# A two-layer network on one core: a row's first stages traced in small pieces between scan items, with chained small matmuls

## The chip, the cores and the metric

The kernel runs on one core of one Trainium2 chip. The metric is the device time of one execution in microseconds (us). Three runs of the kernel before gave 4264.85 to 4278.79 us, with a median of 4274.81 us. The profile is of one more execution, which took 4252.41 us.

The engines are named as the profile does: PE (TensorE, matmuls; PEld its weight loads), DVE (VectorE), ACT (ScalarE), POOL (GpSimd), SP (SyncE, which issues most DMAs). Each takes its own instructions in order and waits for the others on semaphores.

## The reference, cut to what matters

The input `x` has 8 rows of 512 time steps by 256 channels. Two layers add to it four times:

```python
x = x + mamba(ema_gate(x, ...), ...)         # thread X: per row, rows independent
x = x + moe_top2(per_row_linear(x, id7))     # thread Y, first half
x = x + attention(lora_ffn(x, id7), ...)     # thread Y, second half
x = x + moe_top4(per_row_adapter(x, id6))    # top4
```

`ema_gate` has one moving average of the input, a gate, eight modulated moving averages over time that are blended, and a layer norm. `mamba` has a short convolution over time and then a state scan, for 512 channels with 16 states each:

```python
h   = exp(delta[:, None, :] * A) * h + delta * B_t * x_t    # for each of 512 time steps
y_t = einsum('bn,bnd->bd', C_t, h) + D * x_t
```

`lora_ffn` is a two-layer perceptron of 1024 hidden units whose weights get a low-rank correction that depends on the row. `attention` has 8 heads with 64 channels for queries and keys and 256 for values; softmax is over 512 keys. Everything is in float32, apart from a few exact splits into three bfloat16 parts.

## The kernel before, in words

Tiles are 128 channels (or 128 states) on partitions by 512 time steps. A framework traces the kernel as Python, and a scheduler then puts the traced instructions of each engine into an order, by what is ready by its own reckoning of durations and by how early it was traced. The order is fixed when the program is built.

**Thread X** (`thread_x`, L367) does the first addition, row by row. The first stages of a row are `head_a` (L442: gate, eight modulations L475 to L484, layer norm to L513) and `head_b` (L519: convolution L531, gate product, step sizes `dd` by a softplus L559 to L574). The results go to DRAM (`xzs` L535 and L541, `packs` L575). `scan` (L612) then takes the row in 64 items (j, g, k), each 128 lanes of 32 channels by 4 states:

- `begin` (L619) makes the decay `dA` on ACT (L623, Exp) and the input `h` on POOL (L625) from a `packed` tile that a DMA brought (L595); there are 4 buffers for `dA`, 8 for `h`, 5 for `packed`;
- `run` (L645) makes the recurrence on DVE (`tensor_tensor_scan`, L651) and multiplies by C (L652); C comes once per 4 items from a matmul into `c4` (one buffer);
- `add` (L654) folds four items: each item's 4 states are summed by a matmul with a 128x32 matrix into its 32 partitions of `yp` (L660). After the fourth group of states L664 (DVE) and L665 (POOL) make the output `y8`.

`begin` runs two items ahead of `run`. At the end of a row come the product with `W_out`, the sum into `xr` (L685) and the store to `xa` (L686). While row b is scanned, `scan` lets the generator `head(b+1)` advance two steps for each two items; before item 58 it runs that head to its end (`yield from after[0]`). `split3` (L328) makes the three bfloat16 parts.

**Thread Y** (`thread_y`, L711) takes a group of rows, `GROUPS = [[0], [1, 2], [3, 4, 5], [6, 7]]`. It routes tokens to 8 experts (scatters L160 on POOL), runs expert tiles (weights `fw`, L782 to L808), gathers (L323), and then per row does the perceptron (low-rank products into `g`, corrections L838 and L845, products with `wi` and `wo`) and the attention: for each pair of heads, `scores` (L883) makes two products with 64 contracted rows each, the maximum (L893), Exp on ACT with the sum (L896), the reciprocal (L897) and the scaling (L898) on DVE. `turn` transposes (L906, L907), and L923 multiplies by the values; L927 adds to the row.

**Interleaving.** Y of group q is traced while X makes the rows of group q+1. Each generator yields a cost, and the loop at the end of the kernel draws from X as often as keeps the two shares level: `XROW` 269 for a row of X, `YROW` 242 for a row of Y. `filling` (L144) adds DRAM zero fills between X's steps. After X, the last group's Y is traced with the routing of `top4`; then come the top-4 expert tiles and the last gather.

The four folds and the two score products use different column or row groups of the array. Nothing but the trace order keeps them together:

```python
for k in range(4):
    nc.tensor.matmul(
        yps[j][32 * k : 32 * k + 32, :], fold, hs.pop(i + k), start=(g == 0), stop=(g == 3))
```

Of the kernel before, what the change touches and what calls it, by code (L numbers as in the profile page):

```python
# [10 lines left out]
F32 = mybir.dt.float32  # L11
# [6 lines left out]
P = 128  # L18
NB = 8
# [16 lines left out]
XROW, YROW, YGROUP, YTILE, P4ROW = 269.0, 242.0, 20.0, 9.0, 10.0  # L36
# [15 lines left out]
def adaln_attn_ffn_kernel(ctx: ExitStack, tc: tile.TileContext, d: dict, out: bass.AP):  # L52
# [102 lines left out]

    members = {}
# [12 lines left out]
    SYNC = mybir.DependencyInfo(mybir.DependencyClass.Sync, mybir.DependencyReason.DATA)  # L169

# [157 lines left out]
    def split3(pool, src, outs, p0, p1):  # L328

        r = pool.tile([P, T], F32, tag="tr", name="s3_r", bufs=2)[p0:p1, :]  # L330
        m = pool.tile([P, T], BF16, tag="s3_m", name="s3_m")[p0:p1, :]
        nc.scalar.copy(outs[0], src)
        nc.vector.tensor_tensor(r, src, outs[0], ALU.subtract)
        nc.scalar.copy(m, r)
        nc.gpsimd.tensor_tensor(r, r, m, ALU.subtract)
        nc.scalar.copy(outs[1], m)
        nc.scalar.copy(outs[2], r)
# [29 lines left out]
    def thread_x(wp, wk, ps):  # L367
# [74 lines left out]
        def head_a(b):  # L442

            x = rows[b]
            pt = gx()
            mm(pt[:64, :], [(Wn1[:, k, :], x[:, k, :]) for k in range(KC)])
            h1 = wk.tile([64, T], F32, tag="sg", name="h1", bufs=2)
            nc.scalar.activation(h1, pt[:64, :], AF.Gelu, bias=col("bn1", p=64))
            yield 3
            pt = gx()  # L450
            mm(pt[:8, :], [(Wn2, h1)])
            m8 = wk.tile([8, T], F32, tag="tr", name="m8", bufs=2)
            nc.scalar.activation(m8, pt[:8, :], AF.Sigmoid, bias=col("bn2c", p=8))
            split3(wk, m8, [m3[0:8, :], m3[32:40, :], m3[64:72, :]], 0, 8)
            yield 4
            ct = wk.tile([P, KC, T], F32, tag="ct", name="ct")
            for k in range(KC):
                nc.vector.tensor_tensor_scan(
                    ct[:, k, :], alpha[:, 0:1].to_broadcast([P, T]), x[:, k, :], 0.0, ALU.mult, ALU.add)
                yield 1.3  # L460
            gated = wk.tile([P, KC, T], F32, tag="gated", name="gated")
            for e in range(KC):
                pt = gx()
                mm(pt, [(Wg[:, k, ts(e, P)], x[:, k, :]) for k in range(KC)]
                   + [(Wg[:, KC + k, ts(e, P)], ct[:, k, :]) for k in range(KC)])
                sg = wk.tile([P, T], F32, tag="sg", name="sg", bufs=2)
                nc.scalar.activation(sg, pt, AF.Sigmoid, bias=col("bg", e))
                nc.gpsimd.tensor_tensor(gated[:, e, :], x[:, e, :], sg, ALU.mult)
            yield 4
            temporal = wk.tile([P, KC, T], F32, tag="ct", name="temporal")  # L470
            for i in range(8):
                pt = gx()
                mm(pt, [(three[0:72, i : i + 1].to_broadcast([72, P]), m3)])
                gm = wk.tile([P, KC, T], F32, tag="gm", name="gm")
                nc.vector.scalar_tensor_tensor(gm, rep(pt, KC), 0.5, gated, ALU.add, ALU.mult)  # L475
                yield 1.5
                for k in range(KC):
# [8 lines left out]
                    yield 2.2  # L486
            soma = wk.tile([P, KC, T], F32, tag="gm", name="soma")
            for e in range(KC):
                pt = gx()
                mm(pt, [(Wsoma[:, k, ts(e, P)], x[:, k, :]) for k in range(KC)])  # L490
                nc.scalar.activation(soma[:, e, :], pt, AF.Gelu, bias=col("bsoma", e))
            yield 3
            for e in range(KC):
                pt = gx()
                mm(pt, [(Wtemp[:, k, ts(e, P)], temporal[:, k, :]) for k in range(KC)])
                sg = wk.tile([P, T], F32, tag="sg", name="sg", bufs=2)
                nc.scalar.activation(sg, pt, AF.Sigmoid, bias=col("btemp", e))
                nc.gpsimd.tensor_tensor(soma[:, e, :], soma[:, e, :], sg, ALU.mult)
            yield 3
            cen = wk.tile([P, KC, T], F32, tag="cen", name="cen")  # L500
            sq = wk.tile([P, KC, T], F32, tag="gated", name="sq")
            for e in range(KC):
                pt = gx()
                mm(pt, [(Wout[:, k, ts(e, P)], soma[:, k, :]) for k in range(KC)])
                nc.scalar.copy(cen[:, e, :], pt)
                nc.scalar.activation(sq[:, e, :], pt, AF.Square)
                yield 2
            pt = gx()
            mm(pt, [(onesdiv, sq[:, k, :]) for k in range(KC)])
            rstd = wk.tile([P, T], F32, tag="sg", name="rstd", bufs=2)  # L510
            nc.scalar.activation(rstd, pt, AF.Ln, bias=epst)
            nc.scalar.activation(rstd, rstd, AF.Exp, scale=-0.5)
            nc.vector.tensor_tensor(cen, cen, rep(rstd, KC), ALU.mult)  # L513
            yield 3
            rows[b] = cen
            if b + 1 < NB:
                get_row(b + 1)

        def head_b(b):  # L519

            cn = rows[b]
            xc = wk.tile([P, 4, T], F32, tag="xc", name="xc")
            for j in range(4):
                pt = gx()
                mm(pt, [(W_in[:, k, ts(j, P)], cn[:, k, :]) for k in range(KC)])
                xp = xps[j % 2]
                nc.scalar.activation(xp[:, 3:], pt, AF.Identity, bias=wb[:, j : j + 1])
                cv = xc[:, j, :]
                nc.scalar.activation(cv, pt, AF.Identity, scale=col("convw", 4 * j + 3), bias=cb[:, j : j + 1])
                for i in range(3):  # L530
                    nc.vector.scalar_tensor_tensor(  # L531
                        cv, xp[:, i : i + T], col("convw", 4 * j + i), cv, ALU.mult, ALU.add)
                yield 3
            nc.scalar.activation(xc, xc, AF.Silu)
            nc.sync.dma_start(xzs[b % 2][:, :, 0, :], xc)  # L535
            for j in range(4):
                pt = gx()
                mm(pt, [(W_in[:, k, ts(4 + j, P)], cn[:, k, :]) for k in range(KC)])
# [3 lines left out]
            yield 5  # L542
            pt = gx()
            mm(pt[:96, :], [(W_x[:, j, :], xc[:, j, :]) for j in range(4)])
            dt = wk.tile([64, T], F32, tag="dt", name="dt")
            nc.scalar.copy(dt, pt[:64, :])
            bc3 = wk.tile([96, T], BF16, tag="bc3", name="bc3", bufs=2)
            split3(wk, pt[64:96, :], [bc3[64:96, :], bc3[32:64, :], bc3[0:32, :]], 64, 96)
            yield 3

            for j2 in range(2):
                dds, es = [], []
                for j in (2 * j2, 2 * j2 + 1):
                    pt = gx()
                    mm(pt, [(W_dt[:, ts(j, P)], dt)])

                    dd = wk.tile([P, 2, T], F32, tag=("gated", "ct")[j % 2], name="dd")
                    e = wk.tile([P, T], F32, tag="sg", name="sp_e", bufs=2)
                    nc.scalar.activation(e, pt, AF.Abs, bias=col("bdt", j))  # L559
                    nc.vector.tensor_scalar(dd[:, 0, :], pt, col("bdt", j), 0.0, ALU.add, ALU.max)  # L560
                    nc.scalar.activation(e, e, AF.Exp, scale=-1.0)
                    u = dd[:, 1, :]
                    nc.vector.tensor_scalar(u, e, 1.0, None, ALU.add)
                    nc.vector.scalar_tensor_tensor(e, u, 1.0, e, ALU.subtract, ALU.subtract)
                    dds.append(dd)
                    es.append(e)
                yield 3
                for dd in dds:
                    nc.scalar.activation(dd[:, 1, :], dd[:, 1, :], AF.Ln)
                for j, dd, e in zip((2 * j2, 2 * j2 + 1), dds, es):  # L570
                    u = dd[:, 1, :]
                    nc.gpsimd.tensor_tensor(u, u, e, ALU.subtract)
                    nc.gpsimd.tensor_tensor(dd[:, 0, :], dd[:, 0, :], u, ALU.add)
                    nc.gpsimd.tensor_tensor(dd[:, 1, :], dd[:, 0, :], xc[:, j, :], ALU.mult)  # L574
                    nc.sync.dma_start(packs[b % 2][j], dd)  # L575
                yield 3
            rows[b] = bc3

# [33 lines left out]
        def scan(b):  # L612

            bc3 = rows[b]
            items = [(j, g, k) for j in range(4) for g in range(4) for k in range(4)]
            yps, Cs, hs, dAs, xz = {}, {}, {}, {}, {}
            y8 = wk.tile([P, 4, T], F32, tag="y8", name="y8")

            def begin(i):  # L619
                j, g, k = items[i]  # L620
                t = got[b, j, k]
                dA = wk.tile([P, T], F32, tag="dA", name="dA", bufs=4)
                nc.scalar.activation(dA, t[:, 0, :], AF.Exp, scale=A[:, 4 * j + k, g : g + 1])  # L623
# [6 lines left out]
                if j == 0 and g < 3 and k == 1:  # L630
                    get_B4(b, g + 1)
# [570 lines left out]
```

## Time and profile before

| | |
|---|---|
| median of 3 runs | 4274.81 us |
| profiled execution | 4252.41 us, span 4250.6 us |
| mean granted PE clock | 0.889 |
| 512 scans (L651), DVE | 791.0 us, 1571 ns each |
| 512 products with C (L652), DVE | 330.5 us, 672 ns each |
| 512 decays (L623), ACT | 359.8 us, 720 ns each |
| 256 score products (two records each), PE | 210.7 us busy |
| 128 low-rank products (two records each), PE | 63.4 us busy |
| 256 softmax scalings (L898), DVE | 161.8 us, 634 ns each |
| last sum into `xr` of row 0, 1, ... 7 | 406, 750, 1066, 1404, 1749, 2084, 2616, 2938 us |

The span runs from the first to the last instruction. A float32 matmul has two records, one for each pass; busy time is the union of the records, so matmuls that run side by side count once. "Idle before" is idle time of the engine just ahead of an instruction, with what ended it.

### The profile page before, as it was taken

The page shows a single profiled execution, that of the slowest core. Times are in us where ns is not written, and L with a number is a line of the kernel's source. Part 1 is how long each engine was busy: PE and PEld are TensorE (multiplying, and loading weights), DVE is VectorE, ACT ScalarE, POOL GpSimd, SP SyncE. Part 2 cuts the span into 40 slices and gives each one's busy share as a digit, 9 for nine tenths or more (in the row PEclk, how much of TensorE's full clock was granted, in tenths as well). Part 3 has the DMA queues.
Part 4 walks back from the last instruction along what each step waited for, and adds up shares of the span by engine and source line. Part 5 has one row for each costly group of instructions (what it writes and reads, how often), then busy time and mean ns, then how long its engine had stood idle before and what let it go on. Part 6 is the DMA issues. An engine that isn't in the chain of part 4 may idle for free. (4 is left out here: it accounts for less than half of the span.)

```text
span 4250.6 us, 36891 instructions
## 1 busy us (share of the span) xinstructions
PE 3440.5 (81%) x10964; PEld 1694.3 (40%) x10964; DVE 2670.9 (63%) x4290; ACT 1672.2 (39%) x2741; POOL 1565.8 (37%) x1222
## 2 busy tenths in 40 slices
PE   4556686887687888888758899889988999978994
PEld 2111352332254233333327443333456444436773
DVE  4698957886966686796892547575432454443336
ACT  2535463455366346445433443242223233322222
POOL 0456535434635333433542323231043111134552
PEclk7677798988798898999879999899989999989996
DMA  3235455324456423333346312213043312117776
GB/s 105 101 108 180 187 162 170 106 98 156 177 176 209 135 102 118 134 122 109 139 165 234 122 63 77 68 36 104 15 163 136 93 41 70 36 50 245 248 237 224
DMA packets 159372, 554.78 MB, mean 131 GB/s; under 512 B 27730, under 2 KB 34289, under 8 KB 146756
## 3 DMA queue, kind: packets, MB, share of 16 engines
q1 hardware_dynamic: 135076, 501.35, 35.2%
q0 software_dynamic: 24096, 51.08, 3.3%
q8 instruction: 87, 1.43, 0.1%
q14 instruction: 113, 0.93, 0.1%
HBM read 453.00 MB, written 234.82 MB: 162 GB/s over the span
## 5 line engine op out<-in xcount | busy, mean ns | idle before, releaser
L625 POOL TENSOR_TENSOR h<-packed,B 128x512 f32<-128x512 f32 x512 | 792.5, 1570 | 1054.2 <-PE yp L660 746.7
L651 DVE TENSOR_TENSOR_SCAN h<-dA,h 128x512 f32<-128x512 f32 x512 | 791.0, 1571 | 126.3 <-ACT dA L623 67.2
L623 ACT ACTIVATE dA<-packed,Aexp 128x512 f32<-128x512 f32 x512 | 359.8, 720 | 656.4 <-DVE h L651 446.5
L160 POOL DMA_INDIRECT tok<-ys,to_i x310 | 311.9, 1006 | 497.9 <-DVE ys L808 237.7
L660 PE MATMUL yp<-h,fold 128*32 128x512 f32 x1024 | 349.7, 704 | 156.9 <-DVE h L652 140.6
L923 PE MATMUL acc<-aT,V 128*128 128x512 f32 x1024 | 453.4, 597 | 5.3 <-ACT aT L907 3.2
L160 POOL DMA_INDIRECT tab<-row,si x192 | 197.4, 1028 | 465.5 <-issue 210.5
L652 DVE TENSOR_TENSOR h<-h,c 128x512 f32<-128x512 f32 x512 | 330.5, 672 | 29.0 <-PE c L78 28.2
L923 PEld LDWEIGHTS acc<-aT,V 128*128 128x128 f32 x1024 | 193.2, 191 | 245.9 <-issue 235.1
L78 PE MATMUL acc<-wv,c 128*128 128x512 f32 x512 | 270.2, 642 | 0.4
L78 PE MATMUL g<-qk 64*128 64x512 f32 x512 | 210.7, 681 | 54.9 <-ACT ex L896 28.6
L896 ACT ACTIVATE ex<-g,nm 128x512 f32<-128x512 f32 x256 | 173.8, 684 | 157.5 <-DVE nm L893 157.3
L78 PE MATMUL g<-xT,fw 128*128 128x256 f32 x960 | 233.6, 396 | 2.5 <-ACT h L801 1.9
L893 DVE TENSOR_REDUCE nm<-g 128x1 f32<-128x512 f32 x256 | 165.0, 681 | 100.8 <-PE g L78 100.8
L78 PE MATMUL acc<-fw,h 128*128 128x256 f32 x960 | 221.6, 383 | 3.5 <-DVE ys L808 1.8
L78 PEld LDWEIGHTS g<-xT,fw 128*128 128x128 f32 x960 | 188.0, 201 | 39.4 <-issue 6.8
L78 PEld LDWEIGHTS acc<-fw,h 128*128 128x128 f32 x960 | 182.7, 192 | 41.6 <-issue 12.4
L906 PE MATMUL acc<-ident,ex 128*128 128x128 f32 x1024 | 160.3, 286 | 47.9 <-DVE ex L898 16.2
L906 PEld LDWEIGHTS acc<-ident,ex 128*128 128x128 f32 x1024 | 122.6, 146 | 188.4 <-issue 69.3
L660 PEld LDWEIGHTS yp<-h,fold 128*32 128x32 f32 x1024 | 44.7, 115 | 364.1 <-DVE h L652 208.3
L479 DVE TENSOR_TENSOR_SCAN tr<-alpha,gm 128x512 f32<-128x512 f32 x128 | 181.4, 1435 | 5.0 <-POOL y L665 3.5
L78 PE MATMUL g<-xT,mw 128*128 128x256 f32 x760 | 183.1, 385 | 0.0
(280 smaller groups left out, 5458.3 us busy)
## 6 DMA issues: line engine op xcount, KB each, us to landing
fw<-in_fW SPq DMA_DIRECT2D x60, 1154.0 KB
tab<-zeros SPq DMA_DIRECT2D x32, 2112.0 KB
packed<-pack SPq DMA_DIRECT2D x128, 512.0 KB
mw<-in_mW SPq DMA_DIRECT2D x95, 384.0 KB
tab<-zeros SPq DMA_DIRECT2D x16, 2080.0 KB
xt<-tab SPq DMA_DIRECT2D x95, 264.0 KB
xz<-xzs SPq DMA_DIRECT2D x32, 512.0 KB
pack<-dd SPq DMA_DIRECT2D x32, 512.0 KB
```

The source lines that it names most:

```text
L78: nc.tensor.matmul(o, lhsT, rhs, start=(i == 0), stop=(i == len(pairs) - 1))
L160: i = nc.gpsimd.indirect_dma_start(out=table_, out_offset=bass.IndirectOffsetOnAxis(ap=idx, axis=0), in_=src, in_offset=None, bounds_check ...
L479: nc.vector.tensor_tensor_scan(tr, alpha[:, 1 + i : 2 + i].to_broadcast([P, T]), gm[:, k, :], 0.0, ALU.mult, ALU.add)
L623: nc.scalar.activation(dA, t[:, 0, :], AF.Exp, scale=A[:, 4 * j + k, g : g + 1])
L625: nc.gpsimd.tensor_tensor(h, t[:, 1, :], B4s[b, g], ALU.mult)
L651: nc.vector.tensor_tensor_scan(h, dAs.pop(i), h, 0.0, ALU.mult, ALU.add)
L652: nc.vector.tensor_tensor(h, h, Cs[0], ALU.mult)
L660: nc.tensor.matmul(yps[j][32 * k : 32 * k + 32, :], fold, hs.pop(i + k), start=(g == 0), stop=(g == 3))
L893: nc.vector.tensor_reduce(nm, sp, AX.X, ALU.max, negate=True)
L896: nc.scalar.activation(ex, sp, AF.Exp, bias=nm, accum_out=den)
L906: nc.tensor.transpose(tp[:, m, :], ex[:, ts(m, P)], ident)
L923: nc.tensor.matmul(ys[k], V[:, m, C * u + P * k : C * u + P * (k + 1)], aTs[u][:, m, :], start=(u == 0 and m == 0), stop=(u == 1 and m == 3))
```

## The change

1. `head_a` and `head_b` become one generator `head` of about 66 pieces, ended by a bare `yield` each. A matmul, the ACT step on its result and the next DVE or POOL step mostly lie in successive pieces. `split3` is a generator too. `soma` moves into the modulation loop, `get_row` of the next row too.
2. The scan is one loop over the 512 items of all rows. After each item one piece of the heads is traced, after every twelfth two; the folds, the output sum and the end of a row are put into a table `due` and are traced one or more items later, within the next row's items where they fall there. Before item 58 of a row the heads run on until the next row's first `pack` store is traced (`ready`), not to the end of the head.
3. `in_order` gives each instruction of thread X a dependency without a semaphore on the one traced before it on the same engine: the scheduler may not reorder X's instructions.
4. `chain` does the same for the four folds, for the two score products of a turn, and for the low-rank products, which are now traced alternately for `wi` (rows 0 to 31) and `wo` (rows 32 to 63). The first score product also waits for both Exp of the turn before.
5. The softmax scaling goes from DVE to ACT.
6. Buffers: `lora`, `wi`, `wo` share the buffers of `V`, `aT0`/`aT1`, `wv`/`qk`; in X, `m8` moves to `dt`'s, `soma` to `xc`'s, `xr` to `cen`'s. `XROW` is 256; each item yields 4.

```diff
+    def in_order(X):
+        last = {}
+        while True:
+            n = len(nc.cur_bb.bb.instructions)
+            c = next(X, None)
+            for i in nc.cur_bb.bb.instructions[n:]:
+                if i.engine in last:
+                    tc.add_manual_dep(i, last[i.engine].name, NOSYNC)
+                last[i.engine] = i
+            if c is None:
+                return
+            yield c
...
+    def chain(matmuls):
+        for a, b in zip(matmuls, matmuls[1:]):
+            follow(b, a.ins)
...
             for i in range(8):
                 gm = wk.tile([P, KC, T], F32, tag="gm", name="gm")
-                nc.vector.scalar_tensor_tensor(gm, rep(pt, KC), 0.5, gated, ALU.add, ALU.mult)
-                yield 1.5
+                nc.vector.scalar_tensor_tensor(gm, rep(p0, KC), 0.5, gated, ALU.add, ALU.mult)
+                if i in (3, 4):
+                    p0 = gx()
+                    mm(p0, [(Wsoma[:, c, ts(i - 3, P)], x[:, c, :]) for c in range(KC)])
+                yield
...
+            delta(0)
+            yield
+            next(split)
+            soft1(0)
+            delta(1)
+            yield
+            next(split)
+            soft2(0)
+            soft1(1)
+            yield
...
+            if k == 3:
+                due.setdefault(n + 1, []).append(lambda: add(n - 3))
...
+            chain([nc.tensor.matmul(
+                yps[0][32 * k : 32 * k + 32, :], fold, hs.pop(n + k), start=(g == 0), stop=(g == 3)) for k in range(4)])
+            if g == 3:
+                if j == 0:
+                    y8s[b] = wk.tile([P, 4, T], F32, tag="y8", name="y8")
+                due.setdefault(n + 5, []).append(lambda: gate(b, j, n + 6))
...
+        for n in range(N):
+            b, i = divmod(n, 64)
+            if i == 58 and b + 1 < NB:
+                while b + 1 not in ready:
+                    next(H)
+                    yield 0
+            if n + 2 < N:
+                begin(n + 2)
+            run(n)
+            for f in due.pop(n, ()):
+                f()
+            next(H, None)
+            if i % 12 == 4:
+                next(H, None)
+            yield 4
...
+                    pi, po = g(), g()
+                    ms = []
                     for k in range(KC):
-                        mm(pt[:, ts(k, 256)], [(lora[0:32, ts(k, P)], lora[0:32, C + 256 * w : C + 256 * (w + 1)])])
+                        fi, fo = C + 256 * w, C + 256 * w + P * k
+                        ms.append(nc.tensor.matmul(
+                            pi[:, ts(k, 256)], lora[0:32, ts(k, P)], lora[0:32, fi : fi + 256], start=True, stop=True))
+                        ms.append(nc.tensor.matmul(
+                            po[:, ts(k, C)], lora[32:64, fo : fo + P], lora[32:64, 0:C],
+                            start=True, stop=True))
+                    chain(ms)
...
-                        for u in (1, 0):
-                            r0 = 64 * u
-                            mm(sps[u], [(qk[r0 : r0 + 64, 0, ts(i, P)], qk[r0 : r0 + 64, 1, :])])
+                        ms = [nc.tensor.matmul(
+                            sps[u], qk[64 * u : 64 * u + 64, 0, ts(i, P)], qk[64 * u : 64 * u + 64, 1, :],
+                            start=True, stop=True) for u in (1, 0)]
+                        chain(ms)
+                        for e in read:
+                            tc.add_manual_dep(ms[0].ins, e.name, SYNC)
+                        read.clear()
...
-                            nc.vector.tensor_scalar(ex, ex, den, None, ALU.mult)
+                            nc.scalar.activation(ex, ex, AF.Identity, scale=den)
```

## The prediction

> **What bounds it now.** First the page: its totals, and the two groups that the change is about.
>
> ```profile
> span 4250.6 us, 36891 instructions
> ...
> PE 3440.5 (81%) x10964; PEld 1694.3 (40%) x10964; DVE 2670.9 (63%) x4290; ACT 1672.2 (39%) x2741; POOL 1565.8 (37%) x1222
> ...
> L625 POOL TENSOR_TENSOR h<-packed,B 128x512 f32<-128x512 f32 x512 | 792.5, 1570 | 1054.2 <-PE yp L660 746.7
> ...
> L660 PE MATMUL yp<-h,fold 128*32 128x512 f32 x1024 | 349.7, 704 | 156.9 <-DVE h L652 140.6
> ```
>
> 81% of PE says little, since the stages differ. I cut the span where work is handed over: the last sum into `xr` (L685) of rows 0, 2 and 5, at 408, 1068 and 2085 us; the end of X's help and of the third group's attention (about 3100); the last attention sum (3764). I call the stretches A to F and ask for the busy times in each.
>
> ```profile
> 0.00:408.00 408.00, 230.16 (x414) 63.63 (x415) 305.25 (x313) 168.14 (x216) 176.13 (x121) 0.72 0.36 121
> 408.00:1068.00 660.00, 508.19 (x1498) 224.46 (x1498) 499.58 (x631) 320.35 (x485) 294.79 (x206) 0.86 0.43 147
> 1068.00:2085.00 1017.00, 830.86 (x2470) 366.86 (x2469) 774.31 (x1018) 503.74 (x775) 438.97 (x306) 0.89 0.41 142
> 2085.00:3100.00 1015.00, 882.07 (x2832) 426.95 (x2830) 596.18 (x977) 364.79 (x664) 287.06 (x215) 0.94 0.29 100
> 3100.00:3764.00 664.00, 623.67 (x2085) 336.29 (x2086) 286.42 (x707) 199.00 (x372) 162.50 (x164) 0.96 0.26 88
> 3764.00:4250.60 486.60, 365.50 (x1670) 276.13 (x1668) 209.14 (x648) 116.18 (x232) 206.30 (x213) 0.88 0.66 215
> ```
>
> Columns: stretch, its length, busy time of PE, PEld, DVE, ACT, POOL, the granted clock, DMA. The reader is to see three kinds of stage. In B and C (1677 us, five rows of X and three of Y) neither PE (80%) nor DVE (76%) is full: two in-order engines wait for each other. In D and E PE is 87% and 94% busy: PE is the bound. F is expert tiles, in which no edited line stands. So in B and C I look at what DVE waits for, from 408 to 2085:
>
> ```profile
> DVE h L651 <- ACT dA L623: 55.0, 13, 10.8
> DVE dd L560 <- DMA pack<-dd: 39.4, 7, 13.3
> DVE h L651 <- POOL h L625: 35.1, 13, 8.6
> DVE s_r L333 <- ACT bc L332: 26.0, 3, 16.3
> DVE to_m L306 <- DMA xt<-tab: 25.7, 5, 11.4
> DVE xc L531 <- ACT xc L529: 23.6, 9, 6.6
> ...
> DVE y L664 <- PE yp L660: 15.8, 5, 8.4
> ...
> DVE h L652 <- PE c L78: 14.3, 9, 3.2
> DVE dd L560 <- ACT sp_e L559: 14.3, 5, 4.8
> ```
>
> (us in total, times, longest.) DVE is idle for 1677 - 1274 = 403 us. By the lines that wait: 146 us in the head's own chains (dd 39.4 + 14.3 + 5.0, s_r 26.0 + 13.0, xc 23.6, gm 9.9 + 6.7, cen 7.7), 132 us in the scan (55.0 + 35.1 + 15.8 + 14.3, and xr 11.6), the rest, 125, in Y.
>
> **The folds.** A fold has two records, one for each pass. Four folds write four different groups of 32 columns. Two places in the timeline of PE show what their neighbours do to them:
>
> ```profile
> 522.20 1.06 PE L660 MATMUL yp<-h,fold 128*32 128x512 f32 x8
> 523.20 0.39 PE L78 MATMUL gx<-m,three 72*128 72x512 bf16 x1
> ```
> ```profile
> 703.81 2.68 PE L660 MATMUL yp<-h,fold 128*32 128x512 f32 x6
> 709.30 1.05 PE L660 MATMUL yp<-h,fold 128*32 128x512 f32 x2 [2.81 <-DVE h L652]
> ```
>
> Four that stand together take 1.06 us; one alone takes 1.05. So the price is that of a run, not of a fold. In the order of instructions the 512 folds stand in 234 runs before (108 of them single, 45 of four) and in 166 after (88 of four, 39 of three, 38 single). The chain orders the four but doesn't keep strangers out. Per row of X that is 349.7/8 = 43.7 us now and 166 x 1.06/8 = 22 us then: 22 us less. The bounds are 136 us in all (128 whole runs) and 349.7 (all stalls stay).
>
> **Scores and low-rank pairs.** The 256 score products lie in 157 runs before, 133 after; 1.13 us is a full pair (at 781.29). 133 x 1.13 = 150 against 210.7 busy: 7.5 us per row of Y. The low-rank products now alternate between two groups of rows; 63.4 us of busy becomes between 36 (32 groups of 1.13) and 63.4, since 23 of 32 groups are broken into three and one; I take 2 us less per row. The added wait makes the first score product wait for both Exp of the turn before. Behind it stand all later PE instructions. I cost it at nothing: that first product (u = 1) takes the slot of the later of the two Exp already (PE g<-qk after ACT ex is 29.8 us in the whole run). If I am wrong, each of 128 pairs waits one Exp, 0.68 us, at most 88 us.
>
> **Softmax scaling.** DVE loses 256 x 634 ns = 162 us: 23.4 in B, 46.3 in C, 57.2 in D, 34.9 in E (line L898 in these stretches). ACT gains 256 instructions of a form that Y doesn't have; the nearest row is dA, also 128x512 from SBUF with a column as scale, 720 ns (copies take 586, L529 takes 770): 184 us, some 69 of it in B and C, where ACT is 824 of 1677 us busy. The table loads go from 286 to 323 in the order; 37 x 1283 ns = 47 us more. ACT stays under 60% there. The cover is two items of lead of dA; what it costs without it is the fourth case below.
>
> **Pieces and pinned order.** The head's work is the same: the same activations, scans and DMAs are issued, one piece per scan item (5.2 us per item: 1677 / 320). So each of the head's chain waits gets a scan and a product (1.57 + 0.67 us) and what Y puts there as cover. In DVE's new order a piece stands between nearly every scan and its product. I let two thirds of the 146 us go; bounds: all of it, or nothing if the cover is used up by PE's queue. What is late next is the scan's own 132 us (dA, h, c4) and Y's 125; I leave both. Rows already run on (scans of row 1 start 2 us after those of row 0 end), so running on across rows is worth nothing. Row 0 now ends after 71 scans where it ended after 67, 15 us later at 3.8 us per item, but the four items aren't lost: nothing. SP issues the same transfers; pack loads keep their place in the items, pack stores are issued one per piece, and `xz` is loaded three items later, still ten before it is read. On POOL the three instructions of each soft4 (1.4 to 1.5 us each) stand one block per item between the h products instead of two blocks together: POOL is 44% busy there, so nothing. The sum y now comes one item after its folds, which helps the 15.8 us of y, and W_out's products go into the next row's items, where PE has 20% to spare.
>
> **Shared buffers.** lora, wi and wo now wait for V, aT, wv and qk of the row before. The row's gather stands between (L927 last at 1735, L822 at 1756), and a 512 KB transfer lands in 2.66 us (xb, chain of waits): nothing; without the cover 8 x 2 x 2.66 = 43 us.
>
> **The sum**, against the profiled span:
> - A: 408, unchanged, within 20 (PE is idle 44% of it, so folds are worth nothing; the DVE chain is the same).
> - B and C: DVE busy 1274 - 70 = 1204; idle 49 + 132 + 125 = 306; 1510 instead of 1677: 167 less. PE then has 1339 - 5 x 22 - 3 x 9.5 = 1201, 80% of 1510, as now.
> - D: PE 882 - 2 x 22 - 3 x 9.5 = 810; the idle 133 stays: 943. I take 65 less rather than 72, since part of the folds' busy time is waiting.
> - E: two rows of Y, 2 x 9.5 = 19 less at most; I take 16.
> - F: nothing.
>
> 167 + 65 + 16 = 248: span 4003, time 4004 (the execution's time is 1.8 us over its span). The profiled execution took 4252.41 and the median of the runs is 4274.81, 0.53% more: 4025; I say **4025**. Bounds of the same case: half of the idle I remove stays (4075) and, the other way, the scan's idle halves too and D loses 90 (3935).
>
> **Other cases.**
> - *Better.* Head and scan idle both vanish: B and C 1204 + 125 = 1329, 348 less; with D 90, E 16, A 15 the span is 3782, the time 3804. For it: DVE's new order has no two dependent steps of the head side by side. Against it: PE would have to be 90% busy there.
> - *The gain stays off the path.* X keeps its tempo, since POOL's wait for folds (746.7 us) is only 35.1 us of DVE's: DVE and PE just idle more in B and C. Then D gives 30 and E 16: span 4205, time 4228.
> - *The clock.* In slices of 250 us, PE busy 172 and 190 us goes with a granted clock of 0.83 and 0.82, 218 with 0.95, 234 with 0.99. If X's tempo stays, PE falls from 80% to 1201/1677 = 72%, and the clock from about 0.88 to 0.83: 6% of 1201 is 72 us more matmul, on the path of X: 4251 + 72 - 46 = 4277, time 4300 at most; half of it hidden, 4265. The Trainium skill ("TensorE: Matmul & The Clock Gate", Part 1) says that a window of 3.4 us without work halves the clock; by it whole runs of folds, which leave longer gaps, would be a loss where DVE paces. This case's rows agree that a less busy PE has the lower clock; they can't show the window.
> - *Slower.* The order of X's instructions is pinned on every engine. A head activation that waits for its product in PE's queue now holds every dA behind it; the queue holds Y's attention (L923, 16 products of about 0.9 us). ACT's longest waits for a product are 5.1 us (xp), 13.2 (B4), 18.0 (qk). If 7 of the 31 head activations per row that read PSUM come 8 us later than the lead of two items covers, a row loses 56 us against the 33 that I gain (167/5): 23 us slower, 115 in B and C, 46 in D against its 65; E's 16 are kept: 4251 + 115 - 19 - 16 = 4331, time 4355. It decides when the new waits exceed 33 us per row.
>
> **Chances.** Forecast 0.55, better 0.06, off the path 0.17, clock 0.06, slower 0.16. What this kernel's measurement can tell from no change is about 0.3%. Faster by more: 0.55 + 0.06 + 0.17 = 0.78; the same: 0.06; slower: 0.16. The range goes from 3860, between the better case and the forecast's lower bound, to 4300, which takes in the off-path and clock cases.
>
> **What would show it.** Right: fold busy near 180 us, idle before dA-fed scans not larger, a row of X near 300 us instead of 335 in C, PE over 85% in D in a stretch some 65 us shorter, DVE without L898. Wrong: dA waiting on PE products in ACT's list, or rows still 335 us apart with PE at 72%.

## The result, and the profile after

The changed kernel takes 4171.97 us (median of four runs, 4169.97 to 4177.35), beside 4276.8 us for the kernel before on the same chip: a ratio of 0.976, with a 95% interval of 0.9742 to 0.9778. The forecast was 4025. The direction was right, the time lies in the range, and the gain is 105 us where 250 were forecast. The profiled execution has a span of 4168.2 us and a granted clock of 0.875 (0.889 before).

The page of the changed kernel. `L790` is the fold (L660 before), the line with `c<-bc,quads` the product that makes C for four items (`c4`).

```profile
PE 3258.9 (78%) x10964; PEld 1653.5 (40%) x10964; DVE 2635.8 (63%) x4178; ACT 1799.2 (43%) x2890; POOL 1612.5 (39%) x1222
...
L78 PE MATMUL c<-bc,quads 96*128 96x512 bf16 x128 | 57.8, 451 | 209.0 <-DVE h L781 205.5
L790 PE MATMUL yp<-h,fold 128*32 128x512 f32 x1024 | 217.5, 742 | 0.7 <-DVE h L781 0.7
```

The C product in the kernel before (its fold line stands in the prediction):

```profile
L78 PE MATMUL c<-bc,quads 96*128 96x512 bf16 x128 | 55.3, 432 | 48.1 <-DVE h L652 45.9 <-ACT bc L337 1.9
```

PE is 182 us less busy, and 132 of these are the folds (349.7 to 217.5). But read the idle column: PE's wait for DVE's product, 140.6 us at the folds before, has moved to the C product that now stands ahead of them (48.1 us idle before it in the kernel before, 209.0 now). The two idle times together are 205 us before and 210 after. PE meets DVE in another place, for as long.

The same stretches, cut at the same events (last sum into `xr` of rows 0, 2 and 5, end of X's help, last attention sum); the columns are those of the table in the prediction.

```profile
0.00:442.00 442.00, 194.67 (x429) 61.15 (x430) 310.09 (x323) 178.44 (x229) 196.43 (x129) 0.67 0.53 180
442.00:1071.00 629.00, 481.91 (x1522) 221.09 (x1521) 514.54 (x640) 350.60 (x506) 315.14 (x209) 0.85 0.57 205
1071.00:2050.00 979.00, 776.60 (x2489) 356.36 (x2487) 807.71 (x1023) 540.14 (x811) 454.00 (x306) 0.88 0.30 97
2050.00:3009.00 959.00, 822.55 (x2749) 406.08 (x2749) 529.18 (x867) 383.47 (x691) 278.22 (x204) 0.92 0.28 92
3009.00:3684.00 675.00, 618.79 (x2117) 333.89 (x2116) 265.60 (x681) 230.26 (x422) 165.81 (x166) 0.95 0.26 89
```

Cut at the exact ends, the lengths of A to F are 406, 661, 1018, 1007, 670, 489 us before and 442, 629, 979, 959, 672, 487 after. So A loses 36, B and C gain 71 (167 forecast), D gains 48 (65 forecast), E gains nothing (16 forecast). Against the forecast span of 4003 us, 165 us are missing: 96 in B and C, 36 in A, 18 in E and 17 in D, less 2 that F gained. In B and C DVE is idle for 286 us (1608 - 1322); 306 was forecast. But it is busy for 1322, where 1204 was forecast.

DVE's waits in B and C of the changed kernel (us in total, times, longest):

```profile
DVE h L781 <- PE c L78: 55.2, 17, 11.9
DVE to_m L331 <- DMA xt<-tab: 45.3, 8, 11.7
...
DVE h L780 <- ACT dA L752: 19.9, 11, 6.7
...
DVE ct L490 <- DMA pack<-dd: 9.7, 1, 9.7
...
DVE h L780 <- POOL h L754: 7.1, 3, 3.3
```

The head's own waits are gone from the top of the list, as forecast (dd waited 39.4 for the DMA that stores an earlier `dd`; now only `ct`, a scan at the start of a head, waits for that store, 9.7), and the scan waits less for dA and h. What comes up instead is the product's wait for C (14.3 before, 55.2 now) and Y's wait for tokens (25.7, now 45.3).

Two groups of DVE that the prediction did not have:

```profile
L1066 DVE COPY aT<-acc 128x512 f32<-128x512 f32 x152 | 102.3, 679 | 32.4 <-PE acc L1065 28.0 <-remote 4.2
...
L1034 DVE COPY V<-acc 128x512 f32<-128x512 f32 x110 | 74.8, 680 | 24.3 <-PE acc L78 22.1 <-PE g L1042 2.2
```

These copies are written `nc.any`: the scheduler picks the engine. Before, 52 and 62 of them stood on DVE (35.0 and 42.3 us), now 152 and 110. The scaling left DVE with 161.8 us, and copies worth 100 us came in.

### The profile page after: what moved, and what is told of

The parts are those of the page before. It is cut to its first block, busy times and chain, and to the rows that moved or that the text cites. A ratio compares the mean times of both kernels' runs of the same rounds, so it can differ in the third digit from the quotient of the medians.

```text
span 4168.2 us, 36840 instructions
## 1 busy us (share of the span) xinstructions
PE 3258.9 (78%) x10964; PEld 1653.5 (40%) x10964; DVE 2635.8 (63%) x4178; ACT 1799.2 (43%) x2890; POOL 1612.5 (39%) x1222
## 5 line engine op out<-in xcount | busy, mean ns | idle before, releaser
L754 POOL TENSOR_TENSOR h<-packed,B 128x512 f32<-128x512 f32 x512 | 813.0, 1610 | 895.4 <-PE yp L790 536.6
L780 DVE TENSOR_TENSOR_SCAN h<-dA,h 128x512 f32<-128x512 f32 x512 | 791.8, 1546 | 77.1 <-POOL h L754 55.6
L781 DVE TENSOR_TENSOR h<-h,c 128x512 f32<-128x512 f32 x512 | 350.1, 684 | 81.5 <-PE c L78 67.5
L78 PE MATMUL c<-bc,quads 96*128 96x512 bf16 x128 | 57.8, 451 | 209.0 <-DVE h L781 205.5
L790 PE MATMUL yp<-h,fold 128*32 128x512 f32 x1024 | 217.5, 742 | 0.7 <-DVE h L781 0.7
L1057 ACT ACTIVATE ex<-ex,den 128x512 f32<-128x512 f32 x256 | 176.6, 720 | 35.3 <-DVE den L1056 34.5
L1086 DVE TENSOR_TENSOR x<-x,acc 128x512 f32<-128x512 f32 x64 | 43.6, 682 | 231.2 <-PE acc L1082 231.2
L1042 PE MATMUL g<-qk 64*128 64x512 f32 x512 | 159.8, 671 | 33.2 <-ACT ex L1055 20.6
```

The source lines that it names most:

```text
L78: nc.tensor.matmul(o, lhsT, rhs, start=(i == 0), stop=(i == len(pairs) - 1))
L754: nc.gpsimd.tensor_tensor(h, t[:, 1, :], B4s[b, g], ALU.mult)
L780: nc.vector.tensor_tensor_scan(h, dAs.pop(n), h, 0.0, ALU.mult, ALU.add)
L781: product[:] = [nc.vector.tensor_tensor(h, h, Cs[0], ALU.mult).ins]
L790: chain([nc.tensor.matmul(yps[0][32 * k : 32 * k + 32, :], fold, hs.pop(n + k), start=(g == 0), stop=(g == 3)) for k in range(4)])
L1042: ms = [nc.tensor.matmul(sps[u], qk[64 * u : 64 * u + 64, 0, ts(i, P)], qk[64 * u : 64 * u + 64, 1, :], start=True, stop=True) for u in (1 ...
```

## The experiments

The time of the kernel before differs from chip to chip (medians of 4238 to 4277), that of the changed kernel hardly (4168 to 4178 for it and for variants that change nothing). Ratios are to the kernel before on the same chip; I also give us, and say where two kernels shared a chip. The expectations number their theories; these came and fell as the runs went. Theory 1, *returned work:* DVE's busy time sets B and C, and the copies and longer instructions took the gain. Theory 2, *the meeting:* PE's wait at the C product, and DVE's behind it, set the pace. Theory 4 is a pace of X's own, theory 5 that waits only move from one meeting of the queues to the next. In the first runs, rival 2 is that the chains bring the gain and rival 3 that the pinned order holds X up. The contention of DVE and POOL came in with the h products.

**The three chains alone**, in the kernel before (part 4 of the change, with the added wait).

> The kernel before with the three chains alone (folds, the two score products with the added wait for both Exp, low-rank pairs alternating). In the order of instructions the folds stand in 239 runs (before 234, after 166), the scores in 132 (before 157). Theory 1, DVE paces the stretches with X in them, and PE's saved time counts only where PE is the bound: fold busy stays near 350 us, scores save about 50 us of PE, of which the 20 us in the PE-bound stretches count: 4245 to 4265. Rival 2, the chains bring the gain: 4180 to 4210.

4249.74 us, ratio 0.9965 (0.9942 to 0.9987). The folds stand in 239 runs, as before: a chain orders four folds but puts nothing together. E is 14 us shorter, close to the 16 that I gave scores and low-rank pairs.

**The changed kernel without chains** and without the added wait.

```diff
 def chain(matmuls):
-    for a, b in zip(matmuls, matmuls[1:]):
-        follow(b, a.ins)
+    return
```

> The changed kernel without the chains and without the added wait of the first score product (low-rank products stay alternating in the trace). Folds stand in 165 runs (after: 166), scores in 166 (after: 133). Theory 1: only the scores' runs are lost, 20 to 30 us in the PE-bound stretches: 4180 to 4205. Rival 2, the chains bring the gain: 4250 or more.

4216.23 us, 0.9884 (0.9846 to 0.9922), between the two ranges: 1.1% is lost, most of it in E (710 us instead of 672). The folds keep their runs (165). So the pinned order makes the runs, and chains matter for the scores.

**The changed kernel without the pinned order.**

```diff
-        X = filling(in_order(thread_x(
+        X = filling((thread_x(
```

> The changed kernel without the pinned order of X's instructions; pieces, chains and the rest stay. Folds stand in 239 runs again. Theory 1: PE's fold time goes back to about 340 us, which costs the PE-bound stretch that still has X some 35 us and the rest little: 4190 to 4225. Rival 3, the pinned order itself holds X up (row 0 ends 34 us later, PE waits 209 us at the product into c4): faster than after, 4110 to 4150.

4296.15 us, 1.0083 (1.0049 to 1.0118), slower than before, and neither range held. Fold runs are back at 239 and fold busy time at 364 us; B and C take 1695 us (1679 before).

**The scaling back on DVE.**

```diff
-                            nc.scalar.activation(ex, ex, AF.Identity, scale=den)
+                            nc.vector.tensor_scalar(ex, ex, den, None, ALU.mult)
```

> The changed kernel with the softmax scaling back on DVE. In the order 187 copies of aT and V stand on DVE instead of 262 (before: 114). Theory 1, the scheduler gives back to DVE as copies what the scaling took from it: within 20 us of after, 4160 to 4195. Rival, the scaling on ACT carries part of the gain as predicted (about 14 us per row of Y in the stretches with DVE as pace): 4210 to 4240.

4177.93 us, 0.9793 (0.9754 to 0.9831): 6 us more than the changed kernel. The scheduler gives 75 copies back to ACT (187 on DVE instead of 262). The move of 162 us off DVE, the largest single term that I had on DVE, is worth next to nothing in the whole. In the profiled runs B and C do take 24 us more here (1631), with DVE 30 us busier (1352), and the other stretches together 12 less.

**The copies of V and aT pinned to ACT** (two lines, `nc.any.tensor_copy` to `nc.scalar.copy`).

> The changed kernel with the copies of aT and V (512 instructions, of which 262 stand on DVE) written for ACT. Theory 1, DVE paces the stretches with X: DVE loses 54 us there and ACT gains 47; 20 to 50 us faster than the changed kernel, ratio to before 0.965 to 0.972. Rival: ACT, 56% busy there, then holds dA up: no gain or a loss, ratio 0.974 or more.

4167.78 us, 0.9824 (0.9783 to 0.9865). DVE is 50 us less busy in B and C (1272), yet they take 1607 us, as with the copies (1608). So the copies are real work but not what holds the time: DVE was idle 49 us longer. The first theory falls as a rule that B and C follow DVE's busy time.

**C copied to SBUF**, so that the C product does not wait for DVE (ACT copies `c4` into one of two tiles; `xt` and `ys` lose a buffer each to make room).

> The changed kernel with C copied by ACT from c4 into one of two SBUF tiles, so that the product into c4 needs that copy and no longer the last DVE product of the four items before (128 copies, about 75 us of ACT; to make room xt of the first experts' tiles has 3 buffers and their ys 2). Theory 2, PE and DVE meet at c4 every four items and lose time there: PE's wait for h at c4 falls from 209 us to under 40, and the time by 40 to 100 us, ratio 0.952 to 0.966. Theory 1: PE's wait goes to other places, within 20 us of the changed kernel, ratio 0.972 to 0.981.

4287.76 us, 1.0085 (1.0045 to 1.0125); neither range held. PE's wait at the C product is gone, and this stands in its place:

```profile
L783 DVE TENSOR_TENSOR h<-h,cs 128x512 f32<-128x512 f32 x512 | 506.8, 990 | 126.6 <-ACT cs L781 112.8
L792 PE MATMUL yp<-h,fold 128*32 128x512 f32 x1024 | 357.7, 700 | 239.9 <-DVE h L783 218.5
```

The wait went back to the folds, 240 us, and the stalls inside the folds with it. The product takes 990 ns instead of 684 once both operands lie in SBUF. This run changes too much to price the meeting; it shows that the wait moves.

**h on DVE** in the changed kernel.

```diff
-            nc.gpsimd.tensor_tensor(h, t[:, 1, :], B4s[b, g], ALU.mult)
+            nc.vector.tensor_tensor(h, t[:, 1, :], B4s[b, g], ALU.mult)
```

> The changed kernel with the 512 h products on DVE instead of POOL. If a DVE scan that runs beside a POOL instruction is stretched (1.22 us alone and 2.27 beside one, as single instructions of the changed kernel suggest), the mean scan falls from 1546 to about 1230 ns and conv from 959 to about 800; DVE's busy time then rises only by about 512 x 0.69 - 512 x 0.31 = 195 us, and the time by 60 to 150 us. If it isn't, the scan stays at 1546, DVE rises by some 350 us and the time by 200 or more.

4112.88 us, 0.9688 (0.9636 to 0.9741), on the same chip as the run with pinned copies (4167.78): 55 us faster, where I expected a loss. I had seen POOL and DVE slow each other down, but held the 512 products for dearer. The scan falls from 1546 to 1302 ns, the convolution from 970 to 758. DVE's busy time still rises by 41 us in B and C (1363), and they take 26 us less (1582).

**The pinned order alone**, in the kernel before.

> The kernel before with the pinned order of X's instructions alone: coarse steps, old trace order. Folds stand in 154 runs (before 234), table loads 248 (before 286). Theory: pinning pays only with pieces, because here dependent steps of a head follow each other directly on a pinned queue: slower than before by 2% or more, ratio 1.02 to 1.08. Rival: pinning alone brings the gain by whole fold runs and fewer table loads: ratio 0.97 to 0.99.

4371.84 us, 1.0301 (1.0259 to 1.0343). The folds do come in 154 runs, but PE waits 317 us at the C products, and A takes 58 us more, C 50, D 18. Pinning alone costs 3.0%, pieces without pinning (above) 0.8%; together they gain.

**X alone**, in the kernel before, the changed one, and the changed one with h on DVE (everything behind the first addition is left out).

> Thread X of the kernel before alone: it leaves out Y and everything behind it and writes the result of the first addition as its output. In the whole kernel row 0 was scanned beside the head of row 1 alone, without Y, in 245 us. So 150 + 7 x 245 + about 180 for the last row: 2045 us, 1980 to 2120.

> Thread X of the changed kernel alone, with the same left out. Theory 4, X's own pinned chain sets its tempo (a scan of row 0 without Y took 264 us, against 245 before), so that Y beside it is not what kept the gain away: 155 + 7 x 264 + 180, 2150 to 2250, slower than X alone before. Rival: pieces do quicken X by itself, by the DVE idle time that they remove, and only Y's queues hold it back: 1850 to 1980.

> Thread X of the changed kernel alone with the h products on DVE. If POOL beside DVE is a part of X's own chain (it stretches scans and its queue holds dd and h in pinned order), it is faster than X alone after by 5% or more, some 2050; if only the coupling with Y made h on DVE worth 60 us, within 2% of it.

2124.62, 2078.31 and 2126.59 us. None of the three lies in a range that I gave: the first is just above it, the second between theory 4 and its rival, and the third is 2.3% slower than the second. DVE is 82, 85 and 87% busy: alone, X is mostly bound by DVE. Pieces and pinning give 46 us, some 6 per row, where I took 97/5 = 19 per row out of the head's waits: the scan's wait for dA falls from 110.0 to 10.6 us, and its wait for POOL's h rises from 33.4 to 69.0. And h on DVE costs 48 us here, while it gains 55 beside Y. So in the whole kernel X is not at its own pace, and what h on DVE gains there is, by these runs, not work but waiting.

**h on DVE and copies on ACT.**

> The changed kernel with h on DVE and the copies of aT and V on ACT. DVE is then 84% and 87% busy in the stretches with X if the copies stay on DVE; if DVE is now the pace, taking some 50 us of copies from it there gives 25 to 50 us over h on DVE alone: 4060 to 4090, ratio about 0.96. If the fixed meeting of the queues is the pace, as the copies alone showed, within 15 us of it: 4100 to 4125.

4112.38 us, 0.9708 (0.9677 to 0.9739): as with h alone. Again, less work on DVE gives nothing in the whole: with DVE 42 us less busy in B and C (1321) they take 19 us less (1563), and D takes 23 more (957).

**The C product once per row** instead of 16 times (120 of 128 are left out).

> The changed kernel with the product into c4 made once per row instead of once per four items (it leaves out 120 of 128 of them, so that the later items are multiplied with the first group's C). DVE's work is the same. Theory 2, the meeting of PE and DVE at c4 every four items is the pace: 50 us or more faster than the changed kernel. Theory 5, every meeting of the two queues counts and the folds wait for the same product: PE's 205 us move to the folds, within 20 us.

**The head's piece traced before the product** at every fourth item instead of behind it.

> The changed kernel with the piece of the first item of four traced between its scan and its product, so that the product into c4 has the scan and the piece (some 3.5 us instead of 1.5) to be made. Theory 2: DVE's wait for c4 (67 us) nearly gone, 20 to 50 us faster than the changed kernel. Theory 5: that wait gone, but the time within 15 us.

**The changed kernel again**, beside these two.

> The changed kernel itself, for ratios on this chip: 0.974 to 0.978 of the kernel before.

4172.6, 4175.58 and 4170.9 us; 0.9781 (0.9757 to 0.9805), 0.9779 (0.9757 to 0.9801), 0.9778 (0.9758 to 0.9798). The fold of the first of these runs, without most C products:

```profile
L790 PE MATMUL yp<-h,fold 128*32 128x512 f32 x1024 | 324.6, 702 | 169.9 <-DVE h L781 147.5
```

PE waits 148 us for DVE at the folds instead, the folds are busy for 324.6 us instead of 217.5, and the time is the same (B and C 22 us less, D 37 more). The meeting at C is where the wait is seen, not what sets the pace. The second theory falls too, by this run alone: in the second run DVE's wait for c4 hardly fell (58.2 us, 67.5 in the changed kernel), so the piece did not do there what the expectation needs, and that run decides nothing.

**The folds traced one item later** (`n + 1` to `n + 2` in `run`, and the gate behind them).

> The changed kernel with the folds of each item, and the gate behind them, traced one item later. Theory 5 (waits move from one meeting of the queues to the next and the pace does not hang on one place): the ratio stays within 0.005 of 0.978. Rival (in the pinned order the place of the folds in PE's queue sets the pace, since PE meets there what VectorE has just made): one item later gives VectorE 3 us more before PE arrives, the wait of the c4 products on VectorE's products falls from 206 us to under 120 us, and the ratio falls below 0.970.

4168.85 us, 0.9838 (0.9819 to 0.9858): in us the same as the changed kernel on other chips; the ratio, just outside what I gave, is to a kernel before that took 4237.85 on this chip. PE's wait at C is 234 us, not less.

**h on DVE in the kernel before**, no part of the change with it.

> The kernel before with the 512 h products on DVE. If POOL beside DVE costs both kernels alike, it is faster by some 1.4% as the changed kernel was: ratio 0.980 to 0.992. If it became a bound only with pinned order (POOL's queue then holds dd and h in one order), it is the same or slower: 0.998 to 1.03, with DVE busy 100 us more.

4150.98 us, 0.9736 (0.9714 to 0.9758): better than both ranges. One word gains 116 us; the whole change gains 96 on the same chip (4170.9). Two lines of this run's page, and the scan of the kernel before:

```profile
L651 DVE TENSOR_TENSOR_SCAN h<-dA,h 128x512 f32<-128x512 f32 x512 | 631.9, 1243 | 0.7 <-ACT dA L623 0.3
L625 DVE TENSOR_TENSOR h<-packed,B 128x512 f32<-128x512 f32 x512 | 366.3, 717 | 61.8 <-DMA packed<-pack 60.4
```
```profile
L651 DVE TENSOR_TENSOR_SCAN h<-dA,h 128x512 f32<-128x512 f32 x512 | 791.0, 1571 | 126.3 <-ACT dA L623 67.2
```

The scan is 328 ns shorter, and its 126.3 us of idle time are gone (61.8 stand before the h product now). DVE does 366 us of products that POOL did and is as busy as before (2664.6 us, 2670.9 before): its scans give back 159, and other instructions become shorter too, the softmax scaling from 162 to 129 us, the modulation scans from 184 to 156, the blend behind them from 104 to 83. In the kernel before a quarter of the 512 scans take 2147 ns or more; here 95% of them take 1224 or less.

**The same with the three chains.**

> The kernel before with the h products on VectorE and the three chains, without pieces and without the pinned order. Theory 5 (pieces and pinning only win back waits that the contention of VectorE and GpSimd makes or that the loose order makes; once the h products are on VectorE they are worth little): the chains add the 0.35% that they gave alone in the kernel before, so a ratio of 0.968 to 0.972, level with the changed kernel with h on VectorE (0.969). Rival (pieces and pinning carry most of the last gain, and chains do nothing in a loose order): 0.974 or above, as without the chains (0.9736).

4086.21 us, 0.9637 (0.9619 to 0.9656), better than both ranges: the fastest of all, without pieces and pinning, 83 us below the folds-later run on the same chip. By stretches, beside the changed kernel with h on DVE (profiled runs):

| | A | B and C | D | E | F |
|---|---|---|---|---|---|
| kernel before | 406 | 1679 | 1007 | 670 | 489 |
| changed kernel | 442 | 1608 | 959 | 672 | 487 |
| changed, h on DVE | 448 | 1582 | 934 | 658 | 484 |
| before, h on DVE, chains | 393 | 1584 | 962 | 659 | 486 |

In B and C pieces and pinning, with the scaling and the buffers beside them, give 2 us once h is on DVE; with h on POOL they gave 71 (81 beside the kernel with chains alone, 1688). So what they win there is about what the contention had cost; that it is the same waiting is argued, not shown. In A they cost 55, in D the changed kernel (with heads run ahead and the scaling on ACT) is 28 better.

## Why the prediction was wrong

- **The failed step** is the sum for B and C, "DVE busy 1274 - 70 = 1204; idle 49 + 132 + 125 = 306; 1510 instead of 1677: 167 less". Its idle half came out (286). Its busy half is 1322: 70 us went with the scaling, and 54 came with copies, about 36 with heads that run ahead (12 modulation scans more in B and C, 12 fewer in D), and about 30 with instructions that became longer (the convolution's mean 805 to 959 ns in this stretch, the scan's 1523 to 1551). That is the arithmetic of the miss; that the idle half came out is luck, since it did not stay where it was when work was taken away. The step that failed lies in the form of the sum: I took busy time plus a list of waits for the length, as if each term could be taken out while the others stay. Taking 50 us of copies off DVE gave nothing, 42 with h on DVE gave 19, and putting 41 on it gave 26 us.
- **The move to ACT** was priced right, 720 ns forecast and 720 measured (256 in 176.6 us), and bought 6 us by the run that undoes it. I had looked at whether ACT had room, not at which other instructions choose their engine by the room they find.
- **Folds.** 166 runs were right; busy time fell to 217.5 (22 x 8 = 176 forecast). The price of a run was misread: three folds at 703.81 stand in one run and took 2.68 us, not 1.06, because their records start one after another. A run of folds takes 1.31 us on the mean now and took 1.49 before. PE's saving is real where PE is the bound: at the exact cuts D lost 54 us of PE busy time (877 to 823) and 48 in length, 65 forecast. In B and C, PE waits at C instead. I gave the runs to the chain; the pinned order makes them (239 runs with chains alone).
- **Scores.** Busy 159.8 us, 150 forecast; the low-rank products are now two groups (45.3 and 40.5) that overlap, so their 63.4 has no single successor. The added wait costs nothing that shows (PE waits 20.6 us for `ex`, 29.8 before). E gains nothing: chains alone took 14 us off E, the changed kernel without chains has 710. What else made E longer I did not isolate; the variants that keep the chains take 656 to 673 (644 with C copied), so part of it may be the scheduler's spread.
- **A**, costed at nothing, lost 36 us. Row 0 is done after 71 scans, as I had it, but its scans start 5 us later, take 264 us instead of 245, and the end of the row comes 23 us after them instead of 11. I held that the four items "aren't lost"; in A there is no Y that could use them. Pieces without pinning have the loss too (439), pinning without pieces more of it (464), h on DVE does not mend it (448), and without both it is absent (401, 393). How much is the later end of the row and how much the order, no run separates.
- **POOL**, "44% busy there, so nothing", hides a cost as large as the whole gain. Its h products lengthen DVE's scans and hold them up, before and after the change. How much of the gain is the shorter instructions and how much that the scan no longer waits in POOL's queue, no run separates.
- **The rivals.** *Off the path* (4228) had the mechanism for half of it: PE freed in B and C waits instead. *The clock* is seen (A 0.72 to 0.67, D 0.94 to 0.92) but small: B and C, where the case had 0.83, go from 0.86 and 0.89 to 0.85 and 0.88. *Slower* is right that the pinned order costs: alone it takes 129 us (4371.84 against 4243.32 on its chip), 53 of them in B and C and 18 in D, where I had 115 and 46. Its mechanism, dA held up behind a head's activation, does not show there: over the kernel the scan's wait for dA falls from 67.2 to 6.2 us, and PE waits for DVE instead. I had set the gain of the pieces beside it as the likelier case; each alone is a loss, and only together do they gain.

**What stays open.** What paces B and C in the end. The changed kernel, its variants with the copies on ACT, the C product once per row, the piece moved, the folds later or h on DVE, and the two kernels before with h on DVE have 1234 to 1341 us of PE, 1272 to 1363 of DVE and 254 to 774 of POOL in them, and all take 1563 to 1608 us. Apart from h on DVE nothing that was taken away from the changed kernel shortened them by more than 22 us, and D then grew by more than that. X and Y share queues whose order is fixed when the program is built; that waits move in it from one place to another is shown, and that this fixed interleaving is the pace is argued, not shown.

## What to carry to other kernels

Where two in-order engines are each some 80% busy, a wait that is named in the profile is a place, not a price: take it away in a run before you count on it, and do not add up waits and busy times. Before an instruction is moved to free an engine, list what the scheduler may move in. When one form of instruction has a mean far above its shortest time, find what runs beside the long ones first; here that was a single word, worth as much as the whole change. Try such a word in the whole kernel: with X alone it cost 48 us.

## What the hardware showed

DVE and POOL slow each other down when a DVE instruction that takes two operands from SBUF meets a POOL product. The timeline of the changed kernel, in row 0 (start, duration):

```profile
389.01 1.22 DVE L780 TENSOR_TENSOR_SCAN h<-dA,h 128x512 f32<-128x512 f32 x1
...
395.17 1.25 POOL L666 TENSOR_TENSOR dd<-dd,sp_e 128x512 f32<-128x512 f32 x1
395.24 2.27 DVE L780 TENSOR_TENSOR_SCAN h<-dA,h 128x512 f32<-128x512 f32 x1 [4.29 <-POOL h L754]
396.50 2.07 POOL L667 TENSOR_TENSOR dd<-dd 128x512 f32<-128x512 f32 x1
397.62 0.69 DVE L781 TENSOR_TENSOR h<-h,c 128x512 f32<-128x512 f32 x1
```

A scan takes 1.22 us alone and 2.27 when a POOL product has just begun; the POOL product behind it takes 2.07 instead of 1.25. What is added, 1.05 and 0.82 us, is a large part of the other's instruction. The product with C, which reads one operand from PSUM, stays at 0.69 beside the same POOL work; with both operands in SBUF, in the run with C copied, its mean is 990 ns. The Trainium skill ("SBUF — State Buffer", "Who interferes with whom") says that a VectorE instruction with two SBUF inputs contends with a GpSimd instruction that reads SBUF, through a shared pair of ports whose lock is exclusive. These rows agree with it.
